# A sandwich of attention and feed-forward: the small pieces of attention cut in halves over two steps, and put in another order

## The chip, the core and the metric

The kernel runs on one core of a Trainium2 chip. The metric is device time in microseconds. In three runs the kernel before took 2101.5, 2101.69 and 2102.11 us, so its median is 2101.69 us.

The engines are named as in the profile: PE is TensorE (matmuls; PEld are its weight loads), DVE is VectorE, ACT is ScalarE, POOL is GpSimd, SP issues most of the transfers. Each engine works through its own queue in order, and waits at an instruction until what that one needs is there.

## What is computed

Cut to what matters, for x of 8 batches x 512 rows x 512 columns, everything in f32:

```python
def attention(x):                       # 16 heads of 32, rotary part only
    c_kv = x @ W_dkv + b_dkv            # 512 -> 128
    c_q  = x @ W_dq + b_dq              # 512 -> 128
    v = c_kv @ W_uv + b_uv              # 128 -> 512
    q = rotary(c_q @ W_qr + b_qr)       # 128 -> 512
    k = rotary(x @ W_kr + b_kr)         # 512 -> 512
    p = softmax(q @ k.T / sqrt(32))     # per head, 512 x 512
    return (p @ v) @ W_o + b_o

def ffn(x):                             # fwht: Hadamard transform of a row
    x = fwht(x * SU_ug) / 64
    h = silu(x @ W_gate.T * s_gate) * (x @ W_up.T * s_up)      # 512 -> 2048
    return fwht(h * SU_dp) / 64 @ W_down.T * s_down            # 2048 -> 512

x = x + layernorm(attention(layernorm(x)))
x = x + layernorm(ffn(layernorm(x)))
```

## The kernel before

The program has two stages. Attention goes over 8 batches, called blocks here; the feed-forward stage, in which nothing is changed, goes over pairs of batches. The instructions of each engine stand in the order in which the Python code emits them: no scheduler moves them.

**Steps.** A block has 4 groups of 4 heads, and a group has 4 steps c = 0 to 3, one for each 128 keys. So there are 128 steps t, 16 in a block (i = 0 to 15), in one loop (L859). A step of group n does this on PE: the transposed scores of its 128 keys against all 512 queries (`scores_t`, L564 adds the negated maxima as a product of rows, L573 the scores), then the product of the step before's exponentials with the values (`weigh`, L606), and the scores of a later group from which the row maxima come (`row_max`, L527, AHEAD = 6 steps ahead). ACT takes the exponentials (L585), DVE the maxima (L535, two reductions of 128 x 1024 in a step). At c = 2 the sums of exponentials of the group before are taken on PE (`sums`, L623), at c = 3 the maxima are turned into rows (`bias_rows`, L550), from parts which POOL splits at c = 1 (`split`, L543 to L545). POOL adds exponentials at c = 1 and c = 3 (`add_up`, L594: four operations), DVE at c = 0 (`add_pairs`, L599).

**Banks.** Scores go through three tiles of two PSUM banks each (pool `ps_s`), in turn: two for the transposed scores, two for the scores of `row_max`, and sometimes one for a "wide" piece. The second half of the transposed scores therefore needs the tile that the first reduction of the step before has read, and the second half of `row_max` needs the tile that the first exponential has read. All other pieces go through one single bank (pool `ps_f`): flips, sums, bias rows, projections.

**Pieces.** What prepares the next block, and finishes the one before, is cut into pieces that are put between these: four transposes of x (`x_flip`, L394), two compressions to 128 (`compress`, L407, four matmuls each), four keys (`key`, L439, four matmuls each), four queries (`query`, L454, one matmul), four values (`value`, L466, one matmul), four output projections of the block before (`out_proj`, L661 and L662, four matmuls and one in bf16). In addition, 16 pieces of the feed-forward's down weights are transformed during attention (`fold`, L485, one matmul, then four levels on DVE, L493 and L494, and a store). An f32 matmul appears in the trace as two passes, so two records.

Two tables written by hand say which piece stands in which step: BETWEEN (L774), ahead of `row_max` or, for the steps in TWO, as a wide piece after it; and BEHIND (L778), at the end of the step. FIRST_BETWEEN and FIRST_BEHIND are those of block 0, FOLDS and READ place the folds and the loads of their weights. In block 3 this gives, step by step, at the end of the step: value, key, query, value, fold, compression (cq), key, output projection, query + output projection, the same again, fold + output projection, key, query + compression (ckv), value, key, value. Flips stand in steps 0, 1, 4 and 13. Key 3, query 3, values 2 and 3 of a block are made in its own first four steps.

**Rotation.** Queries and keys leave the bank by ACT (L416); `rest` (L418) then shuffles on DVE (L420) and does three operations on POOL (L421 to L423). `rest` is queued in `turns`, and `turn` (L429) empties that queue at two places of each step.

**Around it.** `early` and `later` (L834, L843) place normalization, statistics, the shift (mean times inverse deviation) and the load of x two blocks ahead, and the layernorm, residual and store of the block before. `levels` and `small` are queues of DVE work of which each step takes one.

## Time and profile before

| | us |
|---|---|
| the profiled execution | 2102.66 |
| its span, first to last instruction | 2100.9 |
| attention's 128 steps begin | 46.8 |
| the last of them begins | 890.5 |
| granted TensorE clock, mean | 0.999 of full speed |

The columns of a group's row in the profile are its line and engine, the operation, the tiles written and read, shapes and count, then the busy time in us and the mean length of one in ns, then the idle time of the engine just before the group and what ended it. A row of the timeline has the start, the length, and the merged instructions. Since matmuls overlap, the time a group of them takes is read from its start to the start of the next group.

The mean lengths in attention (from 60 to 880 us) that are used below: DVE shuffle 737 ns, reduction 1217, fold level 0.67 to 0.78 us for its sum and 0.96 to 1.36 for its difference; ACT leaving a bank 687 ns with a bias and 586 without, exponential 1023; POOL add 1386 ns, the three operations of a rotation 1353, 1310 and 1391 (query) and 1436, 1275 and 1457 (key).

### The profile page before, as it was taken

What the parts mean: (1) busy time and instruction counts of PE and PEld (TensorE: products, weight loads), DVE (VectorE), ACT (ScalarE), POOL (GpSimd) and SP (SyncE); (2) the same over time, 40 slices, a digit from 0 to 9 for tenths busy, and PEclk for the clock granted to TensorE, in tenths of its full rate; (3) what the DMA queues carried; (4) which work ended last, traced back from release to release, by engine and by line L of the source; (5) the groups of instructions that cost most, each with busy time, mean ns of one, the idle gap of its engine ahead of it and who ended that gap; (6) DMA issues with size and microseconds to landing.
All of it is one profiled execution on the core that took longest, in us unless ns stands there. A gap on an engine that the chain in (4) does not pass through costs nothing.

```text
span 2100.9 us, 26741 instructions
## 1 busy us (share of the span) xinstructions
PE 2076.8 (99%) x9035; PEld 1057.4 (50%) x9042; DVE 1414.4 (67%) x2356; ACT 745.3 (35%) x1199; POOL 1575.4 (75%) x1629
## 2 busy tenths in 40 slices
PE   8999999999999999999999999999999999999998
PEld 4333333333333333344444677676676766777753
DVE  5698777676767677465545866678866678656542
ACT  3554545555555545522121122222222222222211
POOL 4787979787878889645453678788888879787852
PEclk9999999999999999999999999999999999999999
DMA  3112121212121122237454444444343344444432
GB/s 122 37 31 51 42 54 49 47 51 52 46 57 46 32 66 72 70 104 221 145 166 152 146 143 148 133 138 149 130 157 131 131 137 144 138 158 136 138 112 70
DMA packets 215913, 218.12 MB, mean 104 GB/s; under 512 B 87376, under 2 KB 147920, under 8 KB 215776
## 3 DMA queue, kind: packets, MB, share of 16 engines
q1 hardware_dynamic: 215424, 215.32, 33.2%
q8 instruction: 72, 1.18, 0.2%
q0 software_dynamic: 352, 1.08, 0.1%
q14 instruction: 65, 0.53, 0.1%
HBM read 169.18 MB, written 46.92 MB: 103 GB/s over the span
## 4 chain that ended last, share of the span: by engine, by line
PE 94%; DVE 3%; issue 1%; POOL 1%; ACT 1%; DMA 0%; SPq 0%; POOLq 0%; DVEq 0%; ACTq 0%
PE d L1123 24%; PE psy L1225 18%; PE s L527 6%; PE ops L606 6%; PE ps_k L439 5%; PE ps_y L662 5%; PE t L573 5%; PE u L1106 5%; PE g L1106 4%; PE psz L1516 3%; PE t L564 3%; PE l L623 2%; PE ps_q L454 2%; PE ps_v L466 1%; PE ps_cq L407 1%; PE fxh L207 1%
## 5 line engine op out<-in xcount | busy, mean ns | idle before, releaser
L1225 PE MATMUL psy<-wd,g 128*128 128x512 f32 x896 | 448.9, 592 | 0.0
L535 DVE TENSOR_REDUCE nm<-s 128x2 f32<-128x1024 f32 x256 | 300.8, 1216 | 175.1 <-PE s L527 175.1
L1347 POOL TENSOR_TENSOR pr<-pr,pr 128x512 f32<-128x512 f32 x294 | 391.6, 1357 | 9.0
L594 POOL TENSOR_TENSOR p<-p,p 128x512 f32<-128x512 f32 x244 | 330.2, 1384 | 22.1 <-PE ops L606 22.1
L585 ACT ACTIVATE p<-t 128x1024 f32<-128x1024 f32 x256 | 251.8, 1023 | 89.0 <-PE t L573 89.0
L1123 PE MATMUL d<-xb,wq 128*128 128x256 f32 x992 | 254.2, 380 | 1.9 <-DVE inner L1139 1.4
L1123 PEld LDWEIGHTS d<-tt,wq 128*128 128x128 f32 x864 | 164.0, 190 | 144.4 <-issue 106.0
L1123 PE MATMUL d<-tt,wq 128*128 128x256 f32 x864 | 233.8, 379 | 0.2 <-DVE pr L1144 0.2
L1140 POOL TENSOR_TENSOR pr<-inner 128x256 f32<-128x256 f32 x168 | 126.0, 750 | 138.5 <-DVE inner L1139 105.9
L1123 PEld LDWEIGHTS d<-xb,wq 128*128 128x128 f32 x992 | 186.7, 190 | 62.4 <-issue 30.1
L1225 PEld LDWEIGHTS psy<-wd,g 128*128 128x128 f32 x896 | 169.7, 190 | 49.3 <-issue 29.4
L1136 ACT COPY inner<-d 128x256 f32<-128x256 f32 x168 | 62.6, 373 | 309.6 <-PE d L1123 291.5
L1132 ACT COPY inner<-d 128x256 f32<-128x256 f32 x168 | 62.6, 372 | 300.3 <-PE d L1123 193.2
L527 PE MATMUL s<-kT,qT 32*128 32x512 f32 x1024 | 153.8, 639 | 0.7 <-DVE nm L535 0.7
L573 PE MATMUL t<-qT,kT 32*128 32x512 f32 x1024 | 142.8, 598 | 0.0
L606 PE MATMUL ops<-p,v 128*32 128x512 f32 x1024 | 136.8, 605 | 0.0
L1142 POOL TENSOR_TENSOR pr<-pr,inner 128x256 f32<-128x256 f32 x168 | 136.5, 813 | 0.0
L1123 PE MATMUL d<-T,wq 128*128 128x256 f32 x496 | 127.6, 380 | 0.2
L1144 DVE TENSOR_TENSOR pr<-d,inner 128x256 f32<-128x256 f32 x168 | 70.5, 420 | 75.5 <-PE d L1123 72.9
L439 PE MATMUL ps_k<-xT,wkr_sb 128*128 128x512 f32 x256 | 118.3, 605 | 0.7 <-ACT xT L397 0.7
L662 PE MATMUL ps_y<-wo_sb,oT 128*128 128x512 f32 x256 | 115.8, 593 | 0.9 <-DVE oT L657 0.6
L1135 DVE TENSOR_TENSOR inner<-d,inner 128x256 f32<-128x256 f32 x168 | 70.5, 419 | 62.4 <-PE d L1123 62.0
(219 smaller groups left out, 3263.8 us busy)
## 6 DMA issues: line engine op xcount, KB each, us to landing
wq<-wdeep SPq DMA_DIRECT2D x168, 448.0 KB, 4.2
wd<-wdd SPq DMA_DIRECT2D x112, 256.0 KB, 2.8
wdeep<-w SPq DMA_DIRECT2D x32, 448.0 KB, 5.5
xr<-in_x SPq DMA_DIRECT2D x32, 256.0 KB, 2.8
xin<-x1d SPq DMA_DIRECT2D x32, 256.0 KB, 4.0
xres<-x1d SPq DMA_DIRECT2D x32, 256.0 KB, 3.3
out<-fy SPq DMA_DIRECT2D x32, 256.0 KB, 2.0
rec<-rd SPq DMA_DIRECT2D x124, 64.0 KB, 2.0
```

The lines of the kernel that those rows point to most:

```text
L439: nc.tensor.matmul(ps, lhsT=wkr_sb[:, k, ts(g, P)], rhs=xT[b][:, k, :], start=(k == 0), stop=(k == NK - 1),)
L527: nc.tensor.matmul(sp[j // 2][:, j % 2, :], lhsT=qT[b][rows, g, ts(qc, P)], rhs=kT[b][rows, g, :], start=True, stop=True,)
L535: nc.vector.tensor_reduce(nms[n][:, qc, 2 * h : 2 * h + 2], sp[h], AX.X, ALU.max, negate=True)
L573: nc.tensor.matmul(sp[j // 2][:, j % 2, :], lhsT=kT[b][rows, g, ts(c, P)], rhs=qT[b][rows, g, :], start=False, stop=True,)
L585: nc.scalar.activation(pt[n, c, h], sp[h], AF.Exp)
L594: nc.gpsimd.tensor_add(into, into, pt[n, c, j // 2][:, j % 2, :])
L606: nc.tensor.matmul(o_ps[n][j * DH : (j + 1) * DH, :], lhsT=vv[b][:, c, ds(g * P + j * DH, DH)], rhs=pt[n, c, j // 2][:, j % 2, :], start=( ...
L662: nc.tensor.matmul(ps, lhsT=oT[b][:, k, ts(qc, P)], rhs=wo_sb[:, k, :], start=False, stop=(k == NK - 1),)
L1106: nc.tensor.matmul(ps, lhsT=w[:, SLOT[n], k, :], rhs=rhs[:, k, :], start=k == 0, stop=k == 1)
L1123: nc.tensor.matmul(ps, lhsT=w[:, INNER[m]], rhs=rhs[m], start=True, stop=True)
L1225: nc.tensor.matmul(ys_[t], lhsT=g[:, ts(t, P)], rhs=w, start=n == 0, stop=n == NI - 1)
L1347: nc.gpsimd.tensor_add(pr[n][:, h], pr[a][:, h], pr[b][:, h])
```

## The change

It touches attention alone.

- **Halves.** A new function `half` does 256 of the 512 columns of a fold, value, query, key or compression. `halves` puts one half of a small piece and one half of a large one side by side in one bank, and then copies both out. `both` puts the two halves of such a couple in two consecutive steps.
- **The plan.** BETWEEN, BEHIND, TWO and FOLDS give way to one dictionary `plan` with the places "between" (ahead of `row_max`), "beside" (wide, at the end of the step) and "behind". In blocks 1 to 6 the steps end with: the second half of fold + compression (cq) in step 0; query 0 + key 0 in 1 and 2; query 1 + compression (ckv) in 3 and 4; fold + key 1 in 5 and 6; a value beside an output projection in each of 7 to 10; query 2 + key 2 in 11 and 12; query 3 + key 3 in 13 and 14; the first half of fold + compression (cq) of the block after in 15. All are of the next block. Flips stand in steps 9, 12, 13 and 16 (0 of the next block).
- **Where the work lies.** Nothing of a block's own projections is left for its own steps, from block 2 on. Block 0 has a plan of its own. Block 7 has only output projections, two folds (steps 3 and 8) and the first rows of the feed-forward's input, whose places (`places`) are moved too.
- **Rotation.** `turn(True)` takes one rotation at a time, at up to five places of a group: after the transposed scores in c = 0, 1, 2, and after `row_max` in c = 0 and 3.
- **x.** Its load moves from step 4 to step 14 of the block before, the statistics from steps 6 to 9 to steps 1, 2, 3 and 5 (3 to 6 in block 0), the shift from 11 to 7, the normalizations from 12, 14, 15 and 0 to 8, 11, 12 and 14.
- **Levels.** A fold level is taken at c > 0 (in block 7 in each step), and a small helper no longer in the step of a level.

```diff
-        def turn():
+        def turn(one=False):
             while turns:
                 turns.pop(0)()
+                if one:
+                    return
...
+        HC = S // 2
+        def half(h, ps, fn, b, what):
+            cols = ts(h, HC)
...
+            if fn is query:
...
+                nc.tensor.matmul(
+                    ps, lhsT=wqr_sb[:, ts(what, P)], rhs=cT[b, "cq"][:, cols], start=True, stop=True
+                )
+                def leave():
+                    nc.scalar.activation(
+                        dst[:, cols], ps, AF.Identity, bias=bqs[:, what : what + 1], scale=QSCALE
+                    )
+                    if h == 1:
+                        rotation(qT[b][:, what, :], dst, f"q{b}_{what}")
+                return leave
...
+            for k in range(NK):
+                nc.tensor.matmul(
+                    ps, lhsT=w[:, k, :], rhs=xT[b][:, k, cols], start=k == 0, stop=k == NK - 1
+                )
...
-        BETWEEN = {
-            0: (x_flip, 1, 1), 1: (x_flip, 1, 2), 4: (x_flip, 1, 3),
-            8: (query, 1, 0), 9: (query, 1, 1), 12: (query, 1, 2), 13: (x_flip, 2, 0),
-        }
-        BEHIND = {
-            0: (value, 0, 2), 1: (key, 0, 3), 2: (query, 0, 3), 3: (value, 0, 3),
-            5: (compress, 1, "cq"), 6: (key, 1, 0), 7: (out_proj, -1, 0),
-            8: (out_proj, -1, 1), 9: (out_proj, -1, 2), 10: (out_proj, -1, 3),
-            11: (key, 1, 1), 12: (compress, 1, "ckv"), 13: (value, 1, 0), 14: (key, 1, 2),
-            15: (value, 1, 1),
-        }
...
+        def halves(_, h, small_, large):
+            ps = bank(False, f"ps_{large[0].__name__}_{large[1]}_{large[2]}_{h}")
+            both_ = [(*small_, None, None)[:3], large]
+            for leave in [half(h, ps[:, ts(n, HC)], *which) for n, which in enumerate(both_)]:
+                leave()
...
+        for b in range(NB):
+            for t, i in enumerate((9, 12, 13, 16)):
+                put(b, i, "between", x_flip, b + 2, t)
+        for b in range(1, NB):
+            both(b, 1, (query, b + 1, 0), (key, b + 1, 0))
+            both(b, 3, (query, b + 1, 1), (compress, b + 1, "ckv"))
+            if b < NB - 1:
+                both(b, 5, (fold,), (key, b + 1, 1))
+            for t in range(NT):
+                put(b, 7 + t, "beside", value, b + 1, t)
+                put(b, 7 + t, "behind", out_proj, b - 1, t)
+            both(b, 11, (query, b + 1, 2), (key, b + 1, 2))
+            both(b, 13, (query, b + 1, 3), (key, b + 1, 3))
+            if b < NB - 1:
+                both(b, 15, (fold,), (compress, b + 2, "cq"))
+        put(NB - 1, 3, "behind", fold)
+        put(NB - 1, 8, "beside", fold)
...
+        NORMS = (8, 11, 12, 14)
+        STATS = [(3, 4, 5, 6), (1, 2, 3, 5)]
...
-                if i == 4:
-                    load_x(b + 2, NT)
-                elif 6 <= i < 10:
-                    x_stats(b + 2, i - 6)
-                elif i == 11:
+                if b == 0 and i == 1:
+                    load_x(2, NT)
+                elif i in STATS[b > 0]:
+                    x_stats(b + 2, STATS[b > 0].index(i))
+                elif i == 7:
                     x_shift(b + 2)
+                elif i == 14 and b + 3 < NB:
+                    load_x(b + 3, NT)
...
-            turn()
+            if c < NT - 1:
+                turn(True)
...
-            turn()
+            if c in (0, NT - 1):
+                turn(True)
...
-            if levels and (c > 0 or 0 < i and b < 1):
+            busy_dve = False
+            if levels and (c > 0 or b == NB - 1):
+                busy_dve = len(levels) % 5 != 1
                 levels.pop(0)()
-            if small:
+            if small and not busy_dve:
                 small.pop(0)()
```

## The prediction

> **What bounds the kernel now.** I read the busy table first, then busy time by stage, then TensorE's (PE's) order of time inside one attention block.

> ```profile
> PE 2076.8 (99%) x9035; PEld 1057.4 (50%) x9042; DVE 1414.4 (67%) x2356; ACT 745.3 (35%) x1199; POOL 1575.4 (75%) x1629
> ...
> L535 DVE TENSOR_REDUCE nm<-s 128x2 f32<-128x1024 f32 x256 | 300.8, 1216 | 175.1 <-PE s L527 175.1
> ```

> PE looks full, but ends of matmuls are modelled and overlap their successors, so a wait inside a group of matmuls hides in "busy". The starts tell more. By stage (columns: length, then busy PE, PEld, DVE, ACT, POOL):

> ```profile
> 46.80:148.90 102.10, 98.48 (x577) 32.82 (x578) 79.73 (x97) 52.94 (x68) 82.44 (x79) 1.00 0.13 30
> ...
> 366.20:474.90 108.70, 108.65 (x618) 37.19 (x619) 78.95 (x102) 57.83 (x77) 90.55 (x91) 1.00 0.19 50
> ...
> 800.30:893.00 92.70, 89.48 (x566) 29.17 (x566) 56.66 (x95) 51.49 (x69) 72.34 (x90) 1.00 0.27 73
> ```

> These are batch blocks 0, 3 and 7 of attention; blocks 1 to 6 take 108.1 to 108.7 us each, and from 893 us on nothing changes. Every block is 16 steps. Two steps of block 3 (start, us, group), one behind a heavy piece (ps_k), one behind a light one (ps_v):

> ```profile
> 375.56 3.70 PE L439 MATMUL ps_k<-xT,wkr_sb 128*128 128x512 f32 x8
> 379.19 0.40 PE L564 MATMUL t<-brow,ones_b 32*128 32x512 bf16 x4
> 379.42 1.03 PE L573 MATMUL t<-qT,kT 32*128 32x512 f32 x8
> 380.38 1.06 PE L606 MATMUL ops<-p,v 128*32 128x512 f32 x8
> ```

> ```profile
> 387.18 1.14 PE L527 MATMUL s<-kT,qT 32*128 32x512 f32 x8
> 388.25 1.12 PE L466 MATMUL ps_v<-wuv_sb,ckv 128*128 128x512 f32 x2
> 389.31 0.71 PE L564 MATMUL t<-brow,ones_b 32*128 32x512 bf16 x4
> 389.64 1.24 PE L573 MATMUL t<-qT,kT 32*128 32x512 f32 x8
> 390.81 1.06 PE L606 MATMUL ops<-p,v 128*32 128x512 f32 x8
> ```

> ```profile
> 388.36 2.36 DVE L535 TENSOR_REDUCE nm<-s 128x2 f32<-128x1024 f32 x2 [1.36 <-PE s L527]
> ```

> Behind ps_k, t takes 380.38 - 379.19 = 1.19 us from start to start; behind ps_v 390.81 - 389.31 = 1.50. The second half of t needs a score bank that VectorE (DVE) must have reduced: the first of the two reductions ends at 388.36 + 1.22 = 389.58, and L573 starts at 389.64. So that bank is free 2.45 us after the start of s (387.18). PE is there after s (1.07) and the piece. **A piece under 1.38 us does not shorten the step; one of 1.06 wastes 0.32.**

> **Price list** from such starts: t 1.18, weigh (L606) 1.00, s 1.07, sums 0.86, bias rows 0.33, a flip 0.59; a piece is 0.429 per 512-column pass (an f32 matmul is two) plus 0.20 for entering and leaving the full array. Block 3: 16 x 3.25 + 4 x 0.86 + 4 x 0.33 + 4 x 0.59 + pieces 47.0 (four keys, two compressions, four output projections, four queries, four values, two folds, 16 entries) = 106.1. Six light steps waste 6 x 0.32 = 1.9, and s waits 0.77 in the four steps that have neither flip, sums nor bias rows, for the exponential to free a bank (step 9: 1.34 where step 3 had 1.07):

> ```profile
> 427.27 1.40 PE L527 MATMUL s<-kT,qT 32*128 32x512 f32 x8
> 428.61 1.12 PE L454 MATMUL ps_q<-cq,wqr_sb 128*128 128x512 f32 x2
> ```

> Together 108.7, as measured. At most 2.7 us per block is to be had.

> **The change, part by part.** *Halves.* A small piece (2 passes) and a large one (8) become, in each of two steps, 10 passes over 256 columns. Same columns, same 16 entries per block. The row for such passes is in the feed-forward stage:

> ```profile
> 1202.00 1.46 PE L1123 MATMUL d<-xb,wq 128*128 128x256 f32 x6
> ```

> The next group starts at 1203.30: 216 ns per pass, 1.5 more than half of 429. Seven pairs per block, 140 half passes: +0.2. [...] A paired step has F = 10 x 0.216 + 0.20 = 2.36, 0.98 over the 1.38 that the bank needs, so all six wastes go: -1.9. What is late next is DVE, if its reduction starts over 0.98 us late.

> *Flips moved* to steps 0, 9, 12, 13. The uncovered steps are now 1, 4, 5, 8: 0.26 + 0.18 + 0.26 + 0.18 = 0.88 against 0.77: +0.1. *Values beside output projections* (steps 7 to 10): two passes in front of 8.5, same entry; their copies and the halves' on ScalarE are under 1.4 us per step, done before t ends and the exponentials need it: 0.
> Per block 106.1 + 0.2 + 0.9 = 107.1, thus **-1.6 in each of blocks 2 to 5: -6.4**.

> *Work moved a block ahead.* In blocks 1 to 6 nothing of a block's own projections is left over for its first four steps; block 0 gains two keys' worth, block 7 loses key 3, query 3 and two values. The same prices over blocks 0, 1, 6, 7: light-step waste 2.55 + 1.59 + 1.91 + 3.07 = 9.1 becomes 0.64 + 0 + 0 + 5.1 = 5.7 (steps 0 and 1 of block 7 are now empty, and waste 1.38 each), waits of s 2.5 become 3.3: **-2.6**.

> *DVE's order.* In block 0 PE waits for late reductions, most at step 14, where the queue ahead held a bias helper and a shuffle:

> ```profile
> 132.65 0.39 PE L564 MATMUL t<-brow,ones_b 32*128 32x512 bf16 x2
> 134.31 0.39 PE L564 MATMUL t<-brow,ones_b 32*128 32x512 bf16 x2 [1.27 <-DVE nm L535]
> ```

> That is 1.34 beyond the usual 0.32, with as much again in step 15. One rotation per place, no small helper beside a fold level and only two folds instead of three take that pile apart: **-2.6** (0 to -3). In blocks 1 to 6 the fullest stretch is steps 3 to 5: step 3 puts two shuffles (0.74 each), a statistic and a fold level (0.7 to 1.2 per half) behind two reductions (1.14 apart): 6.3 to 7.3 in a step of 5.9. Lateness 0.7 to 1.7 against 0.98 of cover: 0 to 0.7. Block 7 is fuller: two folds, and steps 0 to 3 ask DVE for about 23 us where PE has 20.4: **+2** (0 to 4).

> *POOL's order.* Rotations (three operations, 4.1) move past the adds of exponentials. From step 3 on the queue holds four adds, three rotations, four adds, then the split that bias rows need in step 7. By mean rows 5.5 + 12.3 + 5.5 + 1.6 = 24.9 us, starting 2.35 into step 3, done at 27.2; PE comes for it at 5.94 + 5.79 + 5.87 + 6.47 + 2.18 = 26.25. By the tightest spacing it is done at 25.7. So 0 to 1.0 per block; with DVE's (the two share one lateness) I take 0.4 in six blocks: **+2.4**, bounds 0 and 8.

> *Queues.* x's load goes from step 4 to step 14 of the block before, x's statistics to 1, 2, 3, 5 and its shift to 7: on SP the load waits for a normalization of the same step, with stores and sums behind it that have a step or more to spare; fold reads come three steps ahead as before: 0. If that cover went, one late flip would cost up to a step's copy, 0.6.

> Sum -6.4 - 2.6 - 2.6 + 2.4 + 2 = **-7.2**. The profiled execution took 2102.66 us around a span of 2100.9, 1.0 above the median of the runs; I subtract from the median 2101.69: **2094.5**.

> **Rivals.** (1) *No new lateness*: DVE and POOL always make it; -11.6, **2090**. For it: POOL adds in block 3 run at 1.24 (4.95 for four). Against: 6.19 for the next four. (2) *Waits exchanged*: DVE lateness at steps 4 to 6 and the split take 1.0 to 1.3 per block, block 7 the whole 4: -11.6 + 7 + 4 = -0.6, or -1.6 at the lower end, **2100.5**. (3) *Slower*: POOL's queue sets the pace of steps 3 to 7, with bias rows (L550) waiting for the split (L545) over 2 us in each of six blocks: from lateness above (11.6 - 2 + 4.2) / 6 = 2.3 us the total is worse than before by more than 0.2%; at 2.6 it is -11.6 + 2 + 15.6 = +6, **2108**. For it: POOL is busy 90.6 of 108.7 us and DVE's two-input operations stretch from 0.41 to 1.5 us beside it. Against: in block 3 the split behind a rotation and four adds ends at 471.0, 1.4 us before PE comes for it at 472.4.

> **Numbers.** Forecast (2091 to 2098) 0.50, rival 1 0.15, rival 2 0.18, rival 3 0.17. Under 0.2% (4.2 us) this kernel can't be told from no change. Faster beyond that: all of rival 1 and most of the forecast, 0.62; same 0.21; slower 0.17. Range 2087 to 2105.

> **What would show it.** Blocks 2 to 5 at 107.1 to 107.9; half passes 216 ns apart; no t group over 1.2 us in steps 1 to 15 of those blocks; L550 at step 7 with a wait under 1 us; block 7's first steps waiting for L535. It is wrong if half passes cost 240 or more, if L550 or L564 waits over 2 us per block, or if blocks 2 to 5 stay at 108.7.

## The result

The changed kernel takes **2128.15 us** (median of 4 runs, 2125.41 to 2132.51), the kernel before 2101.73 beside it: a ratio of 1.0126, with an interval of 1.0114 to 1.0138. It is slower by 26 us where 7 us less were forecast. Its profiled execution, the longest of the four, took 2132.51 us around a span of 2130.7.

From the page of the changed kernel, the busy table and the row of the reductions; then busy time by stage for blocks 0, 3, 4 and 7 (length, then busy PE, PEld, DVE, ACT, POOL, and the granted clock):

```profile
PE 2079.0 (98%) x9452; PEld 1135.2 (53%) x9452; DVE 1401.9 (66%) x2356; ACT 757.1 (36%) x1281; POOL 1565.4 (73%) x1629
...
L617 DVE TENSOR_REDUCE nm<-s 128x2 f32<-128x1024 f32 x256 | 300.3, 1214 | 248.6 <-PE s L609 248.6
```

```profile
46.18:150.90 104.72, 102.46 (x649) 45.45 (x648) 72.02 (x89) 56.63 (x82) 85.59 (x83) 1.00 0.14 36
378.70:491.40 112.70, 109.29 (x677) 48.78 (x676) 77.75 (x102) 59.61 (x88) 88.89 (x91) 0.98 0.20 50
491.40:602.50 111.10, 107.67 (x677) 48.14 (x676) 77.77 (x102) 59.63 (x88) 88.93 (x91) 1.00 0.19 48
824.50:919.67 95.17, 84.17 (x533) 27.33 (x533) 66.25 (x104) 47.60 (x63) 72.80 (x89) 0.96 0.28 71
```

PE's busy time has hardly moved (2076.8 before), DVE's and POOL's went down, and yet each block is longer: 104.7, 115.0, 112.8, 112.7, 111.1, 111.1, 110.8 and 95.2 us for blocks 0 to 7, where they were 102.1, 108.6, four times 108.7, 108.1 and 90.2 (block 7 is counted to the start of its last step). What grew is time in which PE stands still, and block 3 shows a second thing: its clock is 0.98. The feed-forward part is unchanged to 0.8 us (1211.1 from 1210.3).

Which waits? PE's waits within block 3 (line that waits, what it waits for, total, times, longest) name three:

```profile
PE ps_b L632 <- POOL parts L627: 2.3, 2, 1.3
PE t L646 <- DVE nm L617: 0.6, 1, 0.6
PE ps_v L471 <- ACT p L667: 0.5, 1, 0.5
```

Bias rows wait for POOL's split twice, in steps 3 and 7; t waits for a late reduction in step 6; the value of step 7 waits for the exponential. Two steps on PE's timeline, step 4 first (a couple of halves, which waits for nothing), then step 7:

```profile
407.68 0.70 PE L558 MATMUL ps_compress_ckv<-cq,wqr_sb 128*128 128x256 f32 x2
408.21 1.89 PE L584 MATMUL ps_compress_ckv<-xT,wdkv_sb 128*128 128x256 f32 x8
410.04 0.48 PE L646 MATMUL t<-brow,ones_b 32*128 32x512 bf16 x4
```

```profile
424.54 1.06 PE L688 MATMUL ops<-p,v 128*32 128x512 f32 x8
426.89 0.40 PE L632 MATMUL ps_b<-ident_b,parts 128*128 128x128 bf16 x4 [1.29 <-POOL parts L627]
427.21 1.14 PE L609 MATMUL s<-kT,qT 32*128 32x512 f32 x8
428.89 2.08 PE L471 MATMUL ps_v<-wuv_sb,ckv 128*128 128x512 f32 x2 [0.53 <-ACT p L667]
431.18 4.09 PE L744 MATMUL ps_y<-wo_sb,oT 128*128 128x512 f32 x8
```

Step 4 does what was forecast: ten half passes with their entry take 410.04 - 407.68 = 2.36 us, the F of the prediction. Step 7 does not. The value's two passes, usually 1.1 us, took 2.08 us, and three windows beside each other say why:

```profile
425.40:428.80 3.40, 1.67 (x16) 0.54 (x12) 0.41 (x1) 1.81 (x3) 3.03 (x8) 0.99 0.24 39
428.80:432.20 3.40, 3.31 (x5) 1.49 (x6) 3.40 (x7) 0.62 (x2) 3.40 (x4) 0.50 0.00 0
432.20:435.60 3.40, 3.40 (x16) 1.43 (x18) 1.44 (x2) 0.29 (x1) 3.40 (x3) 1.00 0.03 2
```

**After a stretch in which PE was busy for only 1.67 of 3.40 us, the clock is granted at half for the next 3.4 us.** That costs 1.7 us. Blocks 1, 2, 3 and 6 have one such stretch in step 7, blocks 4 and 5 with the same waits have none: step 7 takes 11.9 to 12.1 us in the former (12.4 in block 1), 10.24 in the latter. Its price, the time that the prediction's price list gives it without any wait, is 8.28.

POOL's timeline ahead of that split shows where it is late:

```profile
384.96 2.32 POOL L425 TENSOR_TENSOR rot_q<-rot_q,cs 128x512 f32<-128x512 f32 x1
387.36 2.13 POOL L426 TENSOR_TENSOR qT<-lin_q,rot_q 128x512 f32<-128x512 f32 x1
...
400.33 4.95 POOL L676 TENSOR_TENSOR p<-p,p 128x512 f32<-128x512 f32 x4
405.24 1.27 POOL L424 TENSOR_TENSOR lin_q<-lin_q,cs 128x512 f32<-128x512 f32 x1
...
415.81 1.26 POOL L424 TENSOR_TENSOR lin_q<-lin_q,cs 128x512 f32<-128x512 f32 x1 [1.81 <-DVE rot_q L423]
...
419.61 5.77 POOL L676 TENSOR_TENSOR p<-p,p 128x512 f32<-128x512 f32 x4
...
426.58 0.25 POOL L627 CAST parts<-nm 128x16 bf16<-128x16 f32 x1
```

Additions, the rotations of query 0 and key 0 that ended in one step, 1.81 us of waiting for query 1's shuffle, its rotation, additions, split: from 400.33 to 426.83, 26.5 us. The chain of the prediction was worked out as 24.9, or 23.4 at its tightest. The first two lines belong to the split before it, that of step 3: query 3's rotation took 2.32 and 2.13 us for operations of 1.27; DVE was at pair additions of 3.44 us from 384.92.

DVE's timeline shows why that shuffle, and the reduction that step 6 waits for, came late. Both stand behind pair additions of 3.96 us:

```profile
411.12 3.96 DVE L681 TENSOR_TENSOR p<-p,p 128x1024 f32<-128x1024 f32 x2
...
415.02 0.71 DVE L423 STREAM_SHUFFLE rot_q<-lin_q 128x512 f32<-128x512 f32 x1
415.64 2.33 DVE L617 TENSOR_REDUCE nm<-s 128x2 f32<-128x1024 f32 x2
```

In block 7 it is DVE. PE's timeline, then DVE's:

```profile
833.59 0.39 PE L646 MATMUL t<-brow,ones_b 32*128 32x512 bf16 x2
839.73 0.61 PE L646 MATMUL t<-brow,ones_b 32*128 32x512 bf16 x2 [5.75 <-DVE nm L617]
```

```profile
831.34 4.40 DVE L681 TENSOR_TENSOR p<-p,p 128x1024 f32<-128x1024 f32 x2
835.66 1.48 DVE L501 TENSOR_TENSOR fa<-fz 128x256 f32<-128x256 f32 x1
837.06 1.48 DVE L502 TENSOR_TENSOR fa<-fz 128x256 f32<-128x256 f32 x1
838.46 2.34 DVE L617 TENSOR_REDUCE nm<-s 128x2 f32<-128x1024 f32 x2
```

Pair additions (4.40 for what takes 2.4 alone) and a fold level (2.96 for 0.8) stand ahead of step 1's reduction while POOL rotates query 3 and key 3, left over from block 6. PE waits 5.75 us, and the clock is at half for 6.8 us, from 1.4 us before that wait ends.

To sort these I compare the steps with their prices; what a step takes beyond its price is called its excess. In 77 of the 78 steps of blocks 1 to 6 that are not named here the price holds to 0.02 us. The excess in the changed kernel, in us: steps 3, 6 and 7 of blocks 2 to 5 have +1.1, +1.0 and +2.0 (3.6 with half clock, in blocks 2 and 3); block 0 has about +2 in step 0 and 0.5 or 0.6 in three others; block 1 has +0.4, +1.6 and +4.1 in steps 5, 6 and 7; block 6 has +1.0, none and +3.8 in steps 3, 6 and 7, and +1.1 in step 14; block 7 has +7.4 in step 2 and 0.3 to 1.2 in six others.

### The profile page after: what moved, and what is told of

The parts are those of the page before. It is cut to its first block, busy times and chain, and to the rows that moved or that the text cites. A ratio compares the mean times of both kernels' runs of the same rounds, so it can differ in the third digit from the quotient of the medians.

```text
span 2130.7 us, 27684 instructions
## 1 busy us (share of the span) xinstructions
PE 2079.0 (98%) x9452; PEld 1135.2 (53%) x9452; DVE 1401.9 (66%) x2356; ACT 757.1 (36%) x1281; POOL 1565.4 (73%) x1629
## 3 DMA queue, kind: packets, MB, share of 16 engines
q8 instruction: 75, 1.23, 0.2%
## 4 chain that ended last, share of the span: by engine, by line
PE 81%; POOL 8%; DVE 7%; issue 2%; ACT 1%; DMA 0%; POOLq 0%; SPq 0%; DVEq 0%; ACTq 0%
PE d L1244 23%; PE psy L1346 18%; PE ps_y L744 5%; PE g L1227 5%; PE u L1227 5%; POOL p L676 4%; PE s L609 4%; PE ops L688 3%; PE t L655 3%; PE psz L1637 3%; PE ps_key L584 2%; PE ps_v L471 2%; DVE nm L617 2%; DVE p L681 1%; PE t L646 1%
## 5 line engine op out<-in xcount | busy, mean ns | idle before, releaser
L676 POOL TENSOR_TENSOR p<-p,p 128x512 f32<-128x512 f32 x244 | 310.8, 1304 | 39.9 <-PE ops L688 24.8
L655 PE MATMUL t<-qT,kT 32*128 32x512 f32 x1024 | 137.2, 595 | 0.0
L1281 DVE SCALAR_TENSOR_TENSOR g<-pr,wsu 128x512 f32<-128x512 f32 x96 | 109.3, 1140 | 3.2 <-POOL pr L1468 3.2
```

Of the source, the lines that this page charges most:

```text
L655: nc.tensor.matmul(sp[j // 2][:, j % 2, :], lhsT=kT[b][rows, g, ts(c, P)], rhs=qT[b][rows, g, :], start=False, stop=True,)
L676: nc.gpsimd.tensor_add(into, into, pt[n, c, j // 2][:, j % 2, :])
```

## The experiments

Times are medians beside the kernel before, which had 2101.8 to 2102.9 in these batches.

**1. Rotations only behind a split (step c = 2) or behind the last additions of a group (c = 3 and 0).**

```diff
-            if c < NT - 1:
+            if c in (0, 2):
                 turn(True)
...
-            if c in (0, NT - 1):
+            if c == NT - 1:
                 turn(True)
```

> The changed kernel, with rotations taken at c = 0 and 2 ahead of weigh and at c = 3 after row_max, so never at c = 1 ahead of the adds and the split. POOL theory (the split that bias rows wait for stands behind one rotation too many): the waits of L632 in steps 3 and 7 of blocks 1 to 6 (1.07 and 1.35 to 1.9 us, and the halved clock behind the second) go, blocks at 107 to 108.5, total 2098 to 2103 with block 7's wait left. Rival, DVE theory (DVE's adds of pairs, statistics and fold levels are late of themselves, POOL only follows): step 6 keeps its 1.0 and step 7 over half of its wait, total 2112 or more.

Measured 2171.12 us, 1.0327 (1.0311 to 1.0342). Steps 3 and 7 lost their waits for the split (step 7 keeps 0.6), as the theory says. But step 14 of blocks 1 to 6 gained 7.7 to 9.2 us, step 10 of block 0 gained 6.7, and step 5 of blocks 2 to 5 1.4. ACT's timeline in step 14 of block 3, then POOL's:

```profile
495.28 0.47 ACT L563 ACTIVATE lin_q<-ps_key,bqs 128x256 f32<-128x256 f32 x1 [1.88 <-PE ps_key L584]
502.74 0.47 ACT L589 ACTIVATE lin_k<-ps_key,pv 128x256 f32<-128x256 f32 x1 [6.99 <-POOL qT L426]
503.11 1.93 ACT L667 ACTIVATE p<-t 128x1024 f32<-128x1024 f32 x2
```

```profile
501.44 1.26 POOL L426 TENSOR_TENSOR qT<-lin_q,rot_q 128x512 f32<-128x512 f32 x1
```

An unrotated projection lies in one of three `lin` buffers. Key 3's first half needs the one that query 2 still holds until its rotation, which this rule puts off; ACT waits 6.99 us for it and the exponentials wait behind. So the couples press from two sides: two rotations at once make the split late, and put off, they hold the buffers.

**2. That reading, tested.** The same with `if c in (0, 2) or i == 13`, so that query 2's rotation goes ahead again:

> The run with rotations behind the split, but with query 2's rotation back ahead of step 13's additions. Theory (that run's wait of 8 to 9 us in step 14 is ScalarE waiting for one of three buffers of unrotated projections: key 3's first half needs query 2's): step 14 is back within 0.5 us of its price, steps 3 and 7 stay without their waits, blocks 2 to 5 at 109 to 110, total 2118 to 2124 (block 0 and block 7 keep 6 us each). Rival (the wait is that of the split or of the sums in step 14): step 14 keeps 7 us or more, 2165 or more.

Measured 2119.75, 1.0084 (1.0069 to 1.0099); step 14 is back at its price, and blocks 2 to 5 take 109.1 to 109.2. One part was a miss: step 3's wait for the split came back, with 1.1 us in blocks 2 to 6; why is not shown. Block 0 keeps 6.5 us in step 10, block 7 6.9 in step 2.

**3. A rotation with one POOL operation.** The two products with cosines and sines are left out of every rotation, so its result is not a rotation.

> The changed kernel with two of a rotation's three POOL operations left out (the products with cosine and sine; queries and keys are then not the reference's). POOL theory: 2.7 us less POOL work per rotation, no wait of L632 in blocks 1 to 6, no halved clock there, blocks at 106.5 to 107.5, total 2093 to 2100. Rival (halves, their copies on ACT, or the values beside the output projections cost by themselves): blocks stay at 110 or more, total 2118 or more.

Measured 2101.91, 0.9998 (0.9989 to 1.0007). Blocks 2 to 5 fall to 107.7: POOL's time is what makes steps 3 and 6 and all but 0.6 us of step 7 late. Block 7 keeps +5.6 in step 2: its pair additions fall to 2.35 us, on an idle POOL, but the fold level behind them still takes 2.97 beside POOL's additions.

**4. The old rule for rotations**, all that wait at both places of a step (`turn()` at both).

> The changed kernel with the old rule for rotations: all that are waiting go at each of the two places of every step. Theory (the pairs of a query and a key load POOL in steps 3 to 7, whatever the rule): two rotations stand ahead of step 3's additions, the split of step 7 is still late by 1 us or more, and two shuffles in a row delay a reduction: total 2110 to 2130. Rival (one rotation per place is what makes POOL late): waits of steps 3 and 7 under 0.3 us, total 2091 to 2098.

Measured 2158.93, 1.0270 (1.0253 to 1.0287), worse than either forecast. Step 3's wait went; step 7 kept 1.8 to 2.0 in blocks 2 to 5; and step 15 got 2.9 to 6.0, since query 2 and key 2 now both turn ahead of step 13's additions and split:

```profile
497.14 0.61 PE L632 MATMUL ps_b<-ident_b,parts 128*128 128x128 bf16 x4 [2.88 <-POOL parts L627]
```

One rotation a place is thus a help, not the fault.

**5. Couples made whole**, the small piece in the first step and the large one in the second.

```diff
-                for h in range(2):
-                    put(b, i + h, "behind", halves, 0, h, small_, large)
+                put(b, i, "behind", *small_)
+                put(b, i + 1, "behind", *large)
```

> The changed kernel with its pairs made whole again: the small piece in the first of the two steps, the large one in the second. Theory (the waits come from POOL's queue, because a query and a key that end in the same step hand it two rotations at once): the query's rotation now comes a step (6 us) before the key's, so the waits of the split in steps 3 and 7 shrink to under 1 us, and the light steps waste about 0.32 us each again (1.9 to 2.2 per block): blocks 2 to 5 at 109 to 110, total 2106 to 2114. Rival (half passes have no part in the waits): steps 3, 6 and 7 keep their 1.1, 1.0 and 2.0 to 3.7 us, and the light steps come on top: 2138.

Measured 2124.28, 1.0112 (1.0097 to 1.0127): between the two forecasts. The rotations come a step apart and the waits for the split go, but the light steps are back, and without the cover of halves step 6 has +1.5 beyond a light step's usual waste: pair additions take 4.09 us there beside query 1's rotation. The blocks take 111.1 (107.1, six light steps of 0.32, 0.6 in step 7 and this 1.5), the halves' gain is undone, and the total is hardly better.

**6. Other couples, so that no two rotations end in one step.** All passes and halves stay.

```diff
-            both(b, 1, (query, b + 1, 0), (key, b + 1, 0))
-            both(b, 3, (query, b + 1, 1), (compress, b + 1, "ckv"))
+            both(b, 1, (query, b + 1, 0), (compress, b + 1, "ckv"))
+            both(b, 3, (value, b + 1, 0), (key, b + 1, 0))
...
-            for t in range(NT):
-                put(b, 7 + t, "beside", value, b + 1, t)
+            for t, beside in enumerate([(query, 1), (value, 3), (query, 2), (query, 3)]):
+                put(b, 7 + t, "beside", beside[0], b + 1, beside[1])
...
-            both(b, 11, (query, b + 1, 2), (key, b + 1, 2))
-            both(b, 13, (query, b + 1, 3), (key, b + 1, 3))
+            both(b, 11, (value, b + 1, 1), (key, b + 1, 2))
+            both(b, 13, (value, b + 1, 2), (key, b + 1, 3))
...
-            if c < NT - 1:
+            if (c < NT - 1) if b == 0 else c in (0, 2):
...
-            if c in (0, NT - 1):
+            if c == NT - 1 or b == c == 0:
```

> The changed kernel with the pieces of blocks 1 to 6 mixed so that no two rotations end in one step (query 0 with the compression for the values, values 0, 1, 2 with keys 0, 2, 3, and queries 1, 2, 3 beside output projections), and from block 1 on with rotations only behind a split or behind the last additions of a group. Same passes, same halves. Theory (two rotations at once were what POOL could not place): waits of steps 3, 6 and 7 under 0.3 us, no half clock there, blocks 2 to 5 at 107.0 to 107.6, block 7 at 86 to 92, total 2090 to 2098, faster than both. Rival (POOL's total of additions and rotations, or half passes, is too much in itself): some other step of each block waits 2 us or more, total 2110 or more.

Measured 2101.81, 1.0000 (0.9991 to 1.0009). The waits of steps 3 and 6 are gone, and that for the split in step 7; blocks 2 to 5 take 107.7 and block 7 91.5. PE's waits in block 3 have one line left:

```profile
PE ps_q L459 <- ACT p L667: 0.5, 1, 0.5
```

The blocks' sizes were met to 0.1 us, although that 0.6 in step 7 was not put down; the total misses its forecast, 2090 to 2098, by it (3.6 us in six blocks) and by waits that stayed: in block 0, 1.4 us in step 13 of block 6, 3.7 in step 2 of block 7.

**7. The couples of 6 with the changed kernel's own places for rotations** (both conditions as in the changed kernel).

> The changed kernel with the same new mix of pieces (no two rotations end in one step) but with the changed kernel's own places for rotations. Theory (what matters is that two rotations end together, not the places): waits of steps 3, 6 and 7 under 0.3 us in blocks 2 to 5, apart from the 0.6 us of step 7, total 2101 to 2105. Rival (the places ahead of the additions are what delays the split): step 7 of each block waits 1.3 us or more beyond the 0.6, with half clock in some blocks, total 2110 to 2125.

Measured 2105.04, 1.0013 (1.0006 to 1.0020); blocks 2 to 5 take 108.1 to 108.7. In this order the couples account for 23 of the 26 us lost and the places for 3. It is not so in the other order: the new places with the old couples (run 1) were 43 us slower than the changed kernel, so the places help only once the couples are apart.

**8. What the 0.6 us is.** A piece "beside" is wide: it takes one of the three score banks, which the exponential still reads where a group ends. Run 6, with the piece behind the output projection in steps 7 to 10, and with key 3's rotation for block 7 put off to that block's step 2:

```diff
-            piece("beside", b, i)
-            piece("behind", b, i)
+            for place in ("behind", "beside") if b > 0 and i in OUT else ("beside", "behind"):
+                piece(place, b, i)
...
```

> The run with one rotation a piece, with two more edits. In steps 7 to 10 of blocks 1 to 6 the piece beside an output projection comes after it instead of ahead; and key 3's rotation for block 7 goes at block 7's step 2 instead of ahead of the pair additions of its step 0. Theory: the piece beside takes one of the three score banks, which in step 7, where a group ends, waits 0.6 us for the second exponential; behind the output projection (8 passes, 3.6 us) it waits for nothing: step 7 falls by 0.6 us in each of six blocks, 3.6 us. In block 7 the pair additions no longer share time with a rotation and one shuffle is gone from step 0: step 2's wait falls from 3.7 to 1 to 2 us. Total 2095 to 2098, faster than both by 0.2 to 0.3%. Rival (the 0.6 us is the price of a second entry into the array, not a wait; block 7's wait is VectorE's own work): step 7 and block 7 stay, 2101 to 2103.

Measured **2096.67**, 0.9974 (0.9965 to 0.9984). Step 7 falls by 0.7 and steps 8 to 10 by 0.09 each: 106.7 a block, under the price list. In PE's timeline of step 7 the query no longer waits:

```profile
412.01 3.60 PE L744 MATMUL ps_y<-wo_sb,oT 128*128 128x512 f32 x8
415.44 1.02 PE L459 MATMUL ps_q<-cq,wqr_sb 128*128 128x512 f32 x2
```

Block 7 was missed: step 2 kept 4.2. Its pair additions now run on an idle POOL, in 2.35 us, but the fold level behind them meets POOL's additions (1.48 + 1.48 us).

**9. The same swap alone, in the changed kernel**, to see the clock.

> The changed kernel with one edit: in steps 7 to 10 of blocks 1 to 6 the piece beside an output projection comes after it. Theory (half clock follows a grid window of 3.41 us in which TensorE stood still for some 1.7 us or more, as 1.29 for the split and 0.53 for the bank together do): the 0.53 is gone from step 7, so no half clock is left in blocks 2, 3 and 6; block 1, with its 1.8 us for the split alone, may keep it. Step 7 falls from 11.9 to about 9.5 us in blocks 2, 3 and 6, from 10.2 to 9.5 in 4 and 5: total 2117 to 2121. Rival (one pause of over 1 us is enough): half clock stays in three or four blocks, 2122 to 2126.

Measured 2119.66, 1.0085 (1.0071 to 1.0099). The wait for the split is still 1.29 us in step 7 of block 3, but nothing follows it, and the half clock is gone from blocks 2, 3 and 6; block 1, with 1.8 us, has it. Between the two traces attention falls by 10.9 us: 6 x 0.69 in step 7, 18 x 0.09 in steps 8 to 10, and 3 x 1.7 of clock. Between the medians it is 8.5; the traced execution of the changed kernel is the longest of its four.

**10. The wait filled.** Six 128 x 128 products that nobody reads, ahead of the bias rows of step 7, in the changed kernel.

> The changed kernel with six extra 128 x 128 matmuls on PE (about 1.4 us) ahead of the bias rows of step 7 in blocks 1 to 7, into a bank that nobody reads. Clock theory (PE's pauses in steps 6 and 7 make the granted clock fall to half for 3.4 us): the clock stays full in step 7, passes of 853 ns there become 429, step 7 is 10.0 to 10.6 us in all of blocks 1 to 6 instead of 11.9 to 12.4 in four of them, total 2119 to 2123. Rival (the slow passes come from value and output projection side by side): they stay at 853, total 2128 to 2131.

Measured 2127.99, 1.0122 (1.0107 to 1.0137), a miss. The half clock is gone from blocks 1 to 6, as expected, and step 7 takes 10.5 in all of them (10.7 in block 1). But the products end 0.3 us after the split would have, and in block 7, where there was no such wait, they add 1.6. The spans of the two profiled executions differ by 5.6 us (2130.7 and 2125.1), the medians by 0.2: probably the changed kernel's traced execution, the longest of four, has more half clock than two of its others (granted clocks 0.995, and 0.997, 0.995 and 0.997), which have no trace.

**11. Block 7.** Four runs took work out of its step 0. A fold level (step 0's) left to the next step, in the changed kernel:

> The changed kernel, with no fold level in step 0 of block 7 (and the last fold's load one step later). DVE-pile theory for block 7: the level's two operations (2 x 1.4) no longer stand between the adds of pairs and the next reductions, the 6.1 us wait of L646 in step 2 shrinks to 3 or less and the halved clock behind it goes: block 7 from 95.2 to 88 to 91, total 2121 to 2124. Rival (the adds of pairs alone, stretched to 4.4 us beside POOL, make it late): 1.4 to 3 less at most, total 2125 to 2127.

2129.57, 1.0132 (1.0117 to 1.0147): +3.6 in step 2 and +4.8 in step 3. Levels begun in step 2 and folds two steps later, on top of run 8:

> The faster version of the runs so far (one rotation a piece, beside after) with block 7's fold levels begun in its step 2 instead of step 0 and its two folds two steps later. Theory (in block 7 VectorE has pair additions and a fold level of 3.0 us ahead of step 1's reduction, and step 2 waits 3.7 us for it, which then costs a half clock): step 2 falls from 10.75 to 7 to 8 us and no half clock is left in block 7; of it up to 1 us comes back in steps 3 to 15: total 2093 to 2095. Rival (the wait moves on, as it did when one level was left out of step 0): a later step of block 7 takes 3 us more, total 2096 to 2098.

2097.34, 0.9977 (0.9970 to 0.9985): step 2 is at its price, but steps 3, 4 and 5 take 6.7, 8.2 and 8.6 us where run 8 has 5.3, 5.4 and 6.4, and only 1.1 of it is the fold that moved from step 3 to 5. Both times the wait moved on. So I took work away from DVE: the pair additions of block 6's last group become part of the sums on PE, as block 7's own groups already have it.

```diff
-        APART = {n: (0, 2) for n in range(NG - NK, NG - 2)}
+        APART = {n: (0, 2) for n in range(NG - NK - 1, NG - 2)}
...
-            if n > NG - NK:
+            if n >= NG - NK:
                 if c == 1:
                     sums(n - 1, APART[n - 1])
...
-            if c == 0 and 0 < n <= NG - NK:
+            if c == 0 and 0 < n < NG - NK:
                 add_pairs(n - 1)
```

In the changed kernel:

> The changed kernel with the same one edit: the pair additions of block 6's last group go from VectorE in block 7's step 0 into the sums on TensorE in step 1. Theory (of step 2's 7.4 us the pair additions, 4.4 us beside a rotation, are the larger part and the half clock behind it 2 to 3): step 2 keeps 1 to 3 us, block 7 falls from 95.2 to 90 to 92, total 2123 to 2125. Rival (the fold level alone, or the rotations left over from block 6, hold the reduction up as long): step 2 keeps 5 us or more, total 2127 to 2129.

2127.74, 1.0119 (1.0104 to 1.0135): step 2 is free, but step 3 then waits for the split, behind the leftover rotations:

```profile
845.02 0.47 PE L632 MATMUL ps_b<-ident_b,parts 128*128 128x128 bf16 x4 [3.87 <-POOL parts L627]
```

And on top of run 8, where key 3's is the only rotation left over, and waits until step 2:

> The version with one rotation a piece and beside after, with the pair additions of block 6's last group taken from VectorE in block 7's step 0 and done in the sums on TensorE, as the later groups of block 7 do (eight more passes of 32 columns of weights there, and those sums come in step 1). Theory (block 7's step 2 waits for step 1's reduction behind pair additions and a fold level): step 1 gets longer by the sums, 1.9 us, step 2 loses its sums (0.9), its wait of 3.7 falls to under 1 and its half clock (1.7) goes: block 7 from 91.9 to 88 or 89, total 2093 to 2095. Rival (the fold level, stretched from 0.8 to 3.0 us beside POOL's additions, is late whatever stands ahead of it): step 2 keeps 2 us or more, total 2096 to 2098.

**2094.00**, 0.9959 (0.9947 to 0.9972): block 7 takes 89.3 us and no half clock is left in attention. This version is faster than the kernel before by 0.4% and than the changed one by 1.6% (2094.00 / 2128.15 = 0.984). By stage, in windows that begin 0.6 us ahead of its block 0 and 1.0 ahead of its block 3:

```profile
45.18:149.90 104.72, 102.47 (x654) 45.74 (x651) 72.00 (x89) 56.63 (x82) 85.58 (x82) 1.00 0.14 36
364.90:471.60 106.70, 106.70 (x678) 48.10 (x677) 80.54 (x103) 59.38 (x88) 88.76 (x91) 1.00 0.22 53
```

In block 3 PE is now busy for all of the length, with DVE and POOL as full as in the changed kernel (80.5 and 88.8 us, 77.8 and 88.9 there).

## Why the prediction was wrong

The attention steps were to shrink from 843.7 us by 7.2 to 836.5. The trace has 873.5, **37 us more**: 1.0 in block 0, 5.6 in block 1, 17.7 in blocks 2 to 5, 5.9 in block 6, 6.6 in block 7.

- **Halves, light steps, price list: right.** Ten half passes take 2.36 us; t follows without waiting outside the steps named; run 8 gives blocks 2 to 5 of 106.7 where 107.1 was worked out. The row of the feed-forward stage, 216 ns per half pass, holds in attention too (215 or 216 in step 4 of block 3): run 6, with all its half passes, meets the price list but for step 7's 0.6. (The sum per block, 106.1 + 0.2 + 0.9, is 107.2 and not 107.1; nothing rests on it.)
- **"+2.4" for lateness of POOL and DVE in six blocks: this is the step that failed.** By the excess over the price list it is about 28 us: 5.3 for POOL's split in step 3 (five blocks), 8.7 for it in step 7, 5.9 for DVE's reductions in steps 5 and 6, 1.1 in step 14 of block 6 (the buffer of run 1: PE waits for ScalarE's copy of key 3, and that copy 1.83 us for query 2's rotation), and 6.8 of half clock behind these in this execution. Four things are wrong in that term.
  - Only the split of step 7 was priced. That of step 3 stands behind the rotations of query 3 and key 3 and was put at nothing.
  - The chain to step 7 was started 2.35 us into step 3, as if POOL were free then. It starts 3.1 in (400.33 - 397.24), behind that late split.
  - The chain's rows were summed without a gap. They came to 24.7 us, as summed; but POOL also stood still for 1.81, for a shuffle behind pair additions on DVE. So it was done 29.6 us after the start of step 3, where 27.2 or 25.7 were worked out.
  - DVE's sum for steps 3 to 5 named shuffles, a statistic and a fold level. The pair additions, 3.96 us there, were not in it.
- **"A value beside an output projection: 0": wrong**, 0.6 us in step 7 of six blocks, 3.6 in all. The copy was costed, the bank was not. Runs 8 and 9 show it.
- **"+2" for DVE in block 7 (0 to 4): too small by 6.6.** DVE's 23 us against 20.4 were seen. That pair additions and a fold level would stretch from 3.2 to 7.4 us beside leftover rotations was not, nor that rotations are left over. The runs of 11 and run 8 show that both had to go: without pair additions the wait goes to the split; without the rotations it stays with the level; without both, block 7 is at 89.3, within the 0 to 4.
- **DVE's order in block 0, "-2.6": near.** Steps 14 and 15 lost 0.9 and 0.7 of their 1.3 each; the block is 1.0 longer than worked out.
- **Rival 3 was what happened**, POOL's queue setting the pace with bias rows behind the split, and its own sign ("L550 or L564 waits over 2 us per block") is met with 2.3 in block 3. Its price was 2108: it took the queue's lateness alone, without what DVE, bank and clock add. Against it stood that in the kernel before the split of block 3 was done 1.4 us before PE came. That was a margin of a plan in which rotations come one by one; the change brings them in couples, which the diff tells.

How much of DVE's stretching is POOL's doing can be read from the traces of all 16 kernels, which hold 892 pair additions. The 388 that ran while POOL was idle (at most 5% of their time beside one of its operations) took 1.20 to 1.23 us each. The 288 beside a busy POOL (95% or more) took 1.21 to 2.39, 1.88 in the mean. So the stretch is seen only beside POOL. It goes both ways: POOL's operations of rotations took 1.27 us in the mean away from DVE's two-input operations and 1.71 beside them. Open is which of two that meet gives way, so that the stretch could be worked out ahead.

## What to carry to other kernels

Before making steps equal on the busiest engine, list for each helper engine when each piece hands it work: two pieces that finish together hand over together, and a queue with about 20% of slack on average can come 1 to 2 us late at one place (POOL, busy for 88.9 of the 112.7 us of block 3, let PE wait 1.0 and 1.3 us there). A piece moved to "beside" something costs its buffer (0.53 us in step 7) as well as its passes. And where PE's margin is a few tenths, leave it: several short pauses close together can cost more than their sum, as 1.29 and 0.53 us in step 7 of block 3 did with the 3.4 us of half clock behind them.
